# The last pair of sequences is routed to the experts as two single sequences

## The chip, the cores and the metric

One NeuronCore of a Trainium2 chip runs the kernel. Its engines are TensorE (PE; PEld is its weight load), VectorE (DVE), ScalarE (ACT), GpSimd (POOL) and SyncE (SP); each takes its own instructions strictly in order, and semaphores tie them together. The metric is the time on the device in microseconds (us), where less is better. Lines named as L487 are lines of the kernel before; in the changed kernel the same code stands up to eight lines further down.

## The reference, cut to what matters

Eight sequences of 512 tokens with 128 features go through a block with two halves. The first half is a layer norm with a modulation, four Mamba2 layers (a scan over the tokens) and a residual sum. The second half is a mixture of experts, and the change lies in how its input is made:

```python
h = _layernorm(x, axis=-1) * (1 + cb) + sb
...
normed = hidden_states * jax.lax.rsqrt(var + 1e-08) * norm_weight
shared = jnp.maximum(normed @ sw1 + sb1, 0.0) @ sw2 + sb2
flat = normed.reshape(-1, d)
probs = jax.nn.sigmoid(flat @ router_w.T)
scores, idx = jax.lax.top_k(probs, TOPK)
w = scores / (jnp.sum(scores, axis=-1, keepdims=True) + 1e-06)
...
h = jnp.maximum(jnp.einsum('td,edh->teh', flat, ew1) + eb1[None, :, :], 0.0)
eo = jnp.einsum('teh,eho->teo', h, ew2) + eb2[None, :, :]
routed = jnp.einsum('teo,te->to', eo, comb)
return shared + routed.reshape(b, s, -1)
```

Each of the 4096 tokens goes to two of eight experts and to a shared expert. All is float32.

## The kernel before, in words

**The scan.** A loop over `t` walks through the 128 chunks of each engine's work (8 sequences, 4 chunks of 128 tokens, 4 layers), a few steps of lead and of drain on either side. The order of the instructions on every engine is the order in which this loop writes them (`manual_schedule`). The last chunk's result passes L940 (DVE), L944 (ACT), L955 and L959 (PE), L966 (DVE), L967 (POOL, a power) and L975 (DVE, which adds it to the sequence).

**The route.** When the last layer has finished with a pair of sequences, the generator `rejoin(g)` takes the pair `sets[g]` and does all that stands between scan and experts. It is advanced by one `yield` at a time: in the loop once or twice in each step of the drain, so that its instructions lie between those of the scan, and behind the loop as fast as the others allow. Pair `g` begins at the step `t == NC * (U - B) + NC * (seqs[-1] + 1) + 2`, so the four pairs begin at 106, 114, 122 and 130; the scan's last step is 127. One `rejoin` issues in this order:

- L312 to L316: sums of squares on ACT, then a reciprocal square root `power` (L300 to L305), which from the third pair on is 11 small DVE operations;
- L343, L347, L349: scale (ACT), modulation and residual sum (DVE);
- L355 to L365: statistics and a second root (DVE); L368: the layer norm (ACT); L375: its modulation (DVE);
- L312 again and a third root; L385 (ACT): the rows that go to the experts; L389: the token's number; L395: a second copy of them (DVE);
- L394, L398: the rows transposed (PE) and scaled (ACT); L402: the router's matmuls (PE);
- L424 to L446: the two largest of eight (ACT, DVE); L451 to L464: how many tokens of the set and of earlier sets go to each expert, with the running count in `taken`; L461, L462: a row's place among the tokens of its expert (PE);
- L470 to L480 (DVE): weights and the lists of places `ix`. For each chunk and each of the two experts one scatter is put into the list `scatters`.

**The scatters.** L487 (POOL) writes 128 rows of 130 floats to their places in `xg` in HBM. In the drain one goes out at each step, behind the loop all at once. A pair has 16 of them, all four pairs 64. Rows live in the pool `frow` with two buffers as long as the loop runs, and in `frow2`, also with two, behind it; L380 holds a set back until an older one's scatters have gone out.

**Shared expert.** `shared()` computes it for each routed sequence on PE (L562: hidden layer, L540: second layer) and ACT (L529: ReLU, L533: the result). It is advanced by `serve()` between the steps of `rejoin`.

**Tables and tiles.** When all sets are counted, `tables()` sums up the counts of all tokens (L1131 on PE) and computes on DVE (L1134 to L1163) which expert and which rows each of 39 tiles of 256 rows has; L1168 and L1169 pick the tiles' biases. `fetch(j)` on SP reads a tile's two numbers into registers (L1176, L1177), loads the expert's weights (L1179, L1181), its bias (L1184) and then the rows (L1188). The first three tiles' weights are asked for before the rows of any; the rows need every scatter to have landed. Then, tile by tile, `turn` (L1195), `hidden` (L1206) and `combine` (L1219) run. Only POOL's instructions behind the loop are put in order by the tile scheduler and not by hand: they include two IOTA (L1123, L1125) into memory that the scan's tiles have left, and so wait for these.

Of the kernel before, what the change touches and what calls it, by code (L numbers as in the profile page):

```python
# [8 lines left out]
F32 = mybir.dt.float32  # L9
# [6 lines left out]
P = 128  # L16
# [8 lines left out]
def adaln_mamba_moe(  # L25
# [28 lines left out]
    B, L, DM = x.shape  # L54
# [3 lines left out]
    E, _, FH = ew1.shape  # L58
# [55 lines left out]
    scb = const.tile([P, B, P], F32, name="scb")  # L114
# [102 lines left out]
    fp = ctx.enter_context(tc.tile_pool(name="fp", bufs=1))  # L217
# [13 lines left out]
    taken = [fp.tile([P, E], F32, name="taken0")]  # L231
# [54 lines left out]
        yield  # L286

    hTx, scatters, rowpools, banks, held = {}, [], [frow], [], {}
    sets = [(b, b + 1) for b in range(0, B, 2)]
    routed = set()  # L290

    def power(v, name, on_pool):

# [25 lines left out]
    def rejoin(g):  # L319
# [17 lines left out]
        mine = slice(b0 % 2 * NC, b0 % 2 * NC + n)  # L337
# [39 lines left out]
        rs = yield from mean_squares(h, 1e-8, f"G{g}", on_pool)  # L377
        yield

        while scatters and scatters[0][0] in held.get(len(rowpools), [])[:-1]:  # L380
            yield
        held.setdefault(len(rowpools), []).append(g)
        rows = [rowpools[-1].tile([P, G2, RW], F32, tag=f"row{c}", name=f"row{c}_{g}")[:, :n] for c in range(2)]
        for j in range(n):
            nc.scalar.activation(rows[0][:, j, :DM], h[:, j, :], AF.Copy, scale=rs[:, j : j + 1])  # L385
# [4 lines left out]
        for i, b in enumerate(seqs):  # L390
# [6 lines left out]
            hTx[b] = h[:, t, :].rearrange("p s d -> p (s d)")  # L397
            nc.scalar.activation(hTx[b], pt[:, :L], AF.Copy, scale=nw)  # L398
        yield
        pr = banks[-1](f"pr{g}")  # L400
        for j in range(n):
            nc.tensor.matmul(  # L402
# [10 lines left out]
        def t3(tag):  # L413
            return f2.tile([P, G2, E], F32, tag=tag, name=f"{tag}{g}")[:, :n]

        def t2(tag):
            return f2.tile([P, G2], F32, tag=tag, name=f"{tag}{g}")[:, :n]
# [5 lines left out]
        p = t3("prob")  # L423
# [36 lines left out]
        pp = banks[-1](f"pos{g}")  # L460
        nc.tensor.matmul(pp[:, :m], below, mx.rearrange("p s e -> p (s e)"), start=True, stop=False)  # L461
        nc.tensor.matmul(pp[:, :m], ones, before.rearrange("p s e -> p (s e)"), start=False, stop=True)  # L462
        taken.append(fp.tile([P, E], F32, name=f"taken{g + 1}"))
        nc.vector.tensor_add(taken[g + 1], before[:, n - 1, :], mx[:, n - 1, :])  # L464
        den = t2("den")
        nc.vector.scalar_tensor_tensor(den, m1, 1e-6, m2, ALU.add, ALU.add)
# [8 lines left out]
        for c, oh in enumerate((oh1, oh2)):  # L475
            nc.vector.tensor_mul(oh, oh, pos)
            ix = rowpools[-1].tile([P, G2], mybir.dt.uint32, tag=f"ix{c}", name=f"ix{c}_{g}")[:, :n]
            at = t2(f"at{c}")
            nc.vector.tensor_reduce(at, oh, AX.X, ALU.add)
            nc.vector.tensor_copy(ix, at)  # L480
            for j in range(n):
                scatters.append((g, xg, rows[c][:, j, :], ix[:, j : j + 1], "rows"))
        yield

    def scatter(to, of, ix, group):
# [92 lines left out]
    with ExitStack() as actx:  # L578
# [424 lines left out]
        for t in range(-NC * LEAD - EARLY, NI + 4):  # L1003
            p = t + NC * LEAD
# [16 lines left out]
            for g, seqs in enumerate(sets):  # L1021
                if t == NC * (U - B) + NC * (seqs[-1] + 1) + 2:
                    gens["pairs", g] = rejoin(g)
# [76 lines left out]

    fc = ctx.enter_context(tc.tile_pool(name="fc", bufs=1))
    fh = ctx.enter_context(tc.tile_pool(name="fh", bufs=2))
    rowpools.append(ctx.enter_context(tc.tile_pool(name="frow2", bufs=2)))
    fw3 = ctx.enter_context(tc.tile_pool(name="fw3", bufs=4))
    psT = ctx.enter_context(tc.tile_pool(name="psT", bufs=2, space=PSUM))
    psD = ctx.enter_context(tc.tile_pool(name="psD", bufs=3, space=PSUM))
# [237 lines left out]
```

## Time and profile before

| | |
|---|---|
| median of 4 runs | 1167.01 us (1163.3 to 1168.66) |
| the profiled execution | 1169.04 us, span of its instructions 1167.3 us |
| PE, DVE, ACT, POOL busy | 83%, 73%, 65%, 73% of the span |
| scan and drain | up to about 880 us |
| last routes and scatters | about 880 to 973 us |
| 39 expert tiles | about 977 to 1136 us |
| sums and output | to 1167.3 us |

The page gives the busy time of each engine over the whole span. A table by stretch gives, for each stretch of time, the busy time of each engine with the number of instructions in brackets, then the clock of TensorE that was granted (1.00 is full), the share of the DMA engines' time and what they moved. The list in order of time gives start, duration, engine, line, operation, what it writes and reads, and in square brackets how long the engine was idle before it and what ended that; "issue" is idle time in which the engine waited for nothing that the profile shows, and "remote" an end that it can't assign to an instruction just finished.

### The profile page before, as it was taken

The numbers are of one execution on the slowest core, as the hardware profiler recorded it, in microseconds if no ns is written. First come the engines' busy times: TensorE is split into PE (matmuls) and PEld (weight loads), VectorE is DVE, ScalarE is ACT, GpSimd is POOL, SyncE is SP. The second block draws the span as 40 slices with busy tenths as digits, with TensorE's granted clock in tenths as the row PEclk, the third lists the DMA queues.
The fourth block names the chain that finished last, engine by engine and source line by source line (L and its number), as shares of the span: only waits on it lengthen the run. The fifth ranks groups of instructions, "written<-read, shape, count | busy, mean of one in ns | idle before, by whom it ended". The sixth has DMA issues, their size and how long they took to land. (4 is left out here: it accounts for less than half of the span.)

```text
span 1167.3 us, 21562 instructions
## 1 busy us (share of the span) xinstructions
PE 974.2 (83%) x7130; PEld 738.3 (63%) x7130; DVE 855.9 (73%) x2084; ACT 761.4 (65%) x1641; POOL 856.7 (73%) x937
## 2 busy tenths in 40 slices
PE   4657899989989989899899999877685775999985
PEld 2335666666767767667667676656463554888882
DVE  3768878898898788988988888997554352666653
ACT  4766889778888887888788888767434522333320
POOL 6867978889898798898898887998842533555550
PEclk9767989999999999999999999878867986999997
DMA  5141445546455455363233334424100115787756
GB/s 109 4 138 37 137 118 185 158 128 191 131 192 171 129 169 161 118 209 111 86 134 110 106 107 131 148 93 137 33 23 19 37 44 145 218 218 219 211 145 220
DMA packets 134303, 151.19 MB, mean 130 GB/s; under 512 B 22569, under 2 KB 106697, under 8 KB 134193
## 3 DMA queue, kind: packets, MB, share of 16 engines
q1 hardware_dynamic: 127184, 137.91, 40.0%
q0 software_dynamic: 4672, 9.42, 2.4%
q10 hardware_dynamic: 2336, 2.50, 0.7%
q8 instruction: 56, 0.92, 0.3%
q14 instruction: 55, 0.44, 0.1%
HBM read 120.07 MB, written 29.71 MB: 128 GB/s over the span
## 5 line engine op out<-in xcount | busy, mean ns | idle before, releaser
L668 DVE SCALAR_TENSOR_TENSOR xbc<-px,cw,xbc 128x511 f32<-128x511 f32 (+2 forms) x384 | 286.2, 745 | 35.8 <-ACT xbc L658 28.8
L801 POOL TENSOR_TENSOR dV<-dV,cum 128x1024 f32<-128x1024 f32 x128 | 244.3, 1908 | 5.0 <-DVE xbc L668 4.5
L860 DVE TENSOR_TENSOR dV<-dV,ptx 128x1024 f32<-128x1024 f32 x128 | 155.0, 1211 | 18.1 <-ACT xT L838 17.3
L806 POOL TENSOR_SCALAR_AFFINE_SELECT dV<-dV 128x1024 f32<-128x1024 f32 x128 | 142.2, 1111 | 9.3
L487 POOL DMA_INDIRECT yg<-y,ix x78 | 84.1, 1078 | 85.9 <-DVE y L1230 71.5
L817 ACT ACTIVATE dV<-dV 128x1024 f32<-128x1024 f32 x128 | 134.5, 1051 | 13.5 <-POOL dV L806 13.1
L944 ACT ACTIVATE sq<-g 128x256 f32<-128x256 f32 x128 | 53.0, 414 | 119.3 <-DVE g L940 103.4
L646 PE MATMUL px<-hT,Wi 128*128 128x512 f32 x192 | 104.9, 629 | 15.8 <-DVE xbc L668 14.5
L487 POOL DMA_INDIRECT xg<-row,ix x64 | 63.4, 991 | 62.9 <-ACT hds L529 42.1
L658 ACT ACTIVATE xbc<-px,cbias,cw 128x512 f32<-128x512 f32 x128 | 98.5, 769 | 15.0 <-PE px L646 13.4
L844 POOL TENSOR_TENSOR xd<-xT,dt 128x256 f32<-128x256 f32 x128 | 79.2, 618 | 31.8 <-ACT xT L838 31.3
L869 PEld LDWEIGHTS py<-xbc,st 128*128 128x128 f32 x384 | 60.2, 203 | 62.3 <-issue 49.6
L959 PE MATMUL po<-Wo,g 128*128 128x128 f32 x512 | 89.5, 298 | 0.0
L1212 ACT ACTIVATE hd<-ph,bs 128x256 f32<-128x256 f32 x78 | 32.7, 470 | 83.6 <-PE ph L1206 74.6
L928 PE MATMUL py<-dV,xd 128*32 128x128 f32 x2048 | 85.0, 285 | 0.0
L918 PEld LDWEIGHTS py<-xbc,dg 128*128 128x128 f32 x512 | 80.1, 203 | 7.1 <-issue 1.0
L955 PEld LDWEIGHTS po<-ones,sq 128*128 128x128 f32 x512 | 67.8, 193 | 25.7 <-issue 22.9
L918 PE MATMUL py<-xbc,dg 128*128 128x128 f32 x512 | 82.5, 286 | 0.0
L856 PE MATMUL ptx<-xbc 128*128 128x128 f32 x256 | 55.6, 300 | 30.5 <-DVE dV L860 30.0
L955 PE MATMUL po<-ones,sq 128*128 128x1 f32 x512 | 78.2, 257 | 0.0
L1219 PE MATMUL pe<-w,hd 128*128 128x128 f32 x624 | 75.9, 275 | 0.0
L1206 PE MATMUL ph<-xt,w 128*128 128x256 f32 x312 | 75.1, 385 | 0.1
(252 smaller groups left out, 2358.8 us busy)
## 6 DMA issues: line engine op xcount, KB each, us to landing
dV<-crow SPq DMA_DIRECT2D x128, 512.0 KB
w<-in_L_ffn_ew_dram SPq DMA_DIRECT2D x78, 256.0 KB
xg<-blank SPq DMA_DIRECT2D x64, 260.0 KB
ecum<-crow SPq DMA_DIRECT2D x256, 48.0 KB
rows<-xg SPq DMA_DIRECT2D x39, 130.0 KB
b<-in_L_ffn_eb_dram SPq DMA_DIRECT2D x39, 64.0 KB
x<-in_L_attn_x_dram SPq DMA_DIRECT2D x8, 256.0 KB
md<-mods SPq DMA_DIRECT2D x8, 256.0 KB
```

The source lines that it names most:

```text
L487: i = nc.gpsimd.indirect_dma_start(out=to, out_offset=bass.IndirectOffsetOnAxis(ap=ix, axis=0), in_=of, in_offset=None)
L646: nc.tensor.matmul(px[v, k][:, :L], Wi[l][:, c0 : c0 + P], hT[v], start=True, stop=True)
L658: nc.scalar.activation(xbc[v][:, k, :], px[v, k][:, :L], AF.Identity, bias=cbias[:, l, k : k + 1], scale=cw[:, l, k, KT - 1 : KT],)
L668: nc.vector.scalar_tensor_tensor(xbc[v][:, k, d:], px[v, k][:, : L - d], cw[:, l, k, KT - 1 - d : KT - d], xbc[v][:, k, d:], ALU.mult, ALU ...
L801: nc.gpsimd.tensor_tensor(dV[i], dV[i], cums[g][:, h0 : h0 + NH].unsqueeze(2).to_broadcast([P, NH, Q]), ALU.subtract)
L806: nc.gpsimd.affine_select(out=dV[i], in_=dV[i], pattern=[[0, NH], [1, Q]], compare_op=ALU.is_ge, fill=-200.0, base=0, channel_multiplier=-1,)
L817: nc.scalar.activation(dV[i], dV[i], AF.Exp)
L860: nc.vector.tensor_mul(Ms[i], Ms[i], pg.pop(i).unsqueeze(1).to_broadcast([P, NH, Q]))
L918: nc.tensor.matmul(py[i][:, k, :], dg[l][:, k, :], xbc[u][:, k, t], start=False, stop=True, skip_group_check=True,)
L928: nc.tensor.matmul(py[i][j * HD : (j + 1) * HD, k, :], xd[:, h, :], M[:, h, :], start=False, stop=True, skip_group_check=True,)
L955: nc.tensor.matmul(pp[:, 2 * DM + c : 2 * DM + c + 1], sq[:, k, :], ones[:, 0:1], start=(k == 0), stop=(k == NB - 1))
L959: nc.tensor.matmul(pp[:, c * DM : (c + 1) * DM], g[:, k, :], Wo[l][:, k, :], start=(k == 0), stop=(k == NB - 1))
```

## The change

The last two sequences become sets of their own. There are five sets: three pairs, sequence 6 and sequence 7. Set 3 (sequence 6) begins at `t` = 126 and set 4 (sequence 7) at 130, each with four chunks and eight scatters. All that is issued for each set, such as the roots, the search for the two largest, the counts and the lists, is issued once more, on half as many elements for these two sets.

Three places for rows stand in `frow2`, and a set waits for a place until the set that had it is routed and its scatters have gone out. A set also doesn't start its router's matmuls before the set two ahead of it is routed, so that no more than two are in the buffers of `f2` at a time. The running counts `taken[1:]` lie in columns of `scb`, a tile that the scan's entry has left, instead of in tiles of their own. The two loops that wait do so while the program is written: they set the order of the instructions and are not in the program.

```diff
-    sets = [(b, b + 1) for b in range(0, B, 2)]
-    routed = set()
+    sets = [(b, b + 1) for b in range(0, B - 2, 2)] + [(B - 2,), (B - 1,)]
+    routed, done = set(), {-2, -1}
+    scratch = scb.rearrange("p b q -> p (b q)")
...
-        while scatters and scatters[0][0] in held.get(len(rowpools), [])[:-1]:
-            yield
-        held.setdefault(len(rowpools), []).append(g)
+        while True:
+            mine = held.setdefault(len(rowpools), [])
+            full = mine[-1 - len(rowpools)] if len(mine) > len(rowpools) else -1
+            if full in done and full not in [f[0] for f in scatters]:
+                break
+            yield
+        mine.append(g)
         rows = [rowpools[-1].tile([P, G2, RW], F32, tag=f"row{c}", name=f"row{c}_{g}")[:, :n] for c in range(2)]
...
         yield
+        while g - 2 not in done:
+            yield
         pr = banks[-1](f"pr{g}")
...
-        taken.append(fp.tile([P, E], F32, name=f"taken{g + 1}"))
+        taken.append(scratch[:, g * E : (g + 1) * E])
         nc.vector.tensor_add(taken[g + 1], before[:, n - 1, :], mx[:, n - 1, :])
...
                 scatters.append((g, xg, rows[c][:, j, :], ix[:, j : j + 1], "rows"))
+        done.add(g)
         yield
...
-    rowpools.append(ctx.enter_context(tc.tile_pool(name="frow2", bufs=2)))
+    rowpools.append(ctx.enter_context(tc.tile_pool(name="frow2", bufs=3)))
```

What this makes of the order on the engines: on POOL the scatters of the second pair that are still left at the loop's end stand nine (before: ten) ahead of the two IOTA and five behind them, then L967 and two more (before: L967 and then six). Then come 16 scatters of the third pair, eight of sequence 6 and eight of sequence 7. On PE the positions of sequence 6 (L461, L462) stand right behind those of the third pair, and sequence 7's transposition, router and positions follow between blocks of the shared expert. DVE routes sequence 6 ahead of the third pair as far as the two largest, and issues its lists right behind the third pair's. SP's order is unchanged.

## The prediction

> **What bounds the kernel now.** I read the page, then a table by stretch behind the scan, then the waits and the instructions in order of time there. The page shows busy engines, and that is an average over stages: the table shows 923 to 973 us, where nothing is full.
>
> ```profile
> span 1167.3 us, 21562 instructions
> core 0: us, PE busy (x) PEld busy (x) DVE busy (x) ACT busy (x) POOL busy (x), PEclk, DMA share, GB/s
> 913.00:923.00 10.00, 9.52 (x63) 7.26 (x62) 2.95 (x14) 7.64 (x24) 7.67 (x8) 1.00 0.15 47
> 923.00:936.00 13.00, 5.23 (x25) 3.90 (x24) 0.00 (x0) 0.12 (x1) 7.65 (x8) 0.75 0.14 46
> 949.00:957.00 8.00, 7.19 (x64) 7.00 (x63) 7.38 (x26) 1.13 (x2) 6.44 (x6) 1.00 0.13 43
> 957.00:973.00 16.00, 0.00 (x0) 0.00 (x0) 3.18 (x6) 0.58 (x1) 9.57 (x10) 0.60 0.46 127
> 973.00:981.00 8.00, 4.16 (x12) 3.15 (x13) 0.00 (x0) 1.74 (x4) 0.00 (x0) 0.52 0.72 208
> ```
>
> From 923 to 936 PE issues 25 matmul records instead of some 80, and waits for nothing that the profile names ("issue"). The waits and the order of time tell with what this goes:
>
> ```profile
> PE pes L540 <- issue: 7.8, 11, 1.8
> ...
> 877.75 0.16 DVE L966 TENSOR_SCALAR rg<-po 128x2 f32<-128x2 f32 x1 [9.34 <-remote]
> 877.80 0.28 POOL L1123 IOTA ahead<- 128x128 f32 x1 [1.58 <-remote]
> 878.67 0.72 POOL L967 TENSOR_TENSOR rg<-rg,mhalf 128x2 f32<-128x2 f32 x1
> 879.43 0.61 DVE L975 SCALAR_TENSOR_TENSOR h<-po,rg,h 128x128 f32<-128x128 f32 x2 [1.51 <-POOL rg L967]
> 913.04 0.96 POOL L487 DMA_INDIRECT xg<-row,ix  x1 [26.09 <-ACT hds L529]
> 931.98 0.96 POOL L487 DMA_INDIRECT xg<-row,ix  x1 [0.30 <-issue]
> 935.88 0.58 ACT L533 COPY h<-pes 128x512 f32<-128x512 f32 x1 [14.45 <-remote]
> 948.98 0.96 POOL L487 DMA_INDIRECT xg<-row,ix  x1 [16.05 <-ACT hds L529]
> 968.63 0.95 POOL L487 DMA_INDIRECT xg<-row,ix  x1 [0.30 <-issue]
> 972.14 0.58 ACT L533 COPY h<-pes 128x512 f32<-128x512 f32 x1 [18.17 <-remote]
> 973.33 1.36 SPq L1188 DMA_DIRECT2D rows<-xg  x3
> 976.70 1.12 PE L1195 MATMUL pt<-ident,rows 128*128 128x128 f32 x4 [20.51 <-DMA rows<-xg]
> ```
>
> The reader should see a pattern, three times. POOL issues a run of scatters (L487) every 1.26 us; some us into the run nobody sees any more what PE has finished; 1.5 to 2.9 us after the run ends all of it is seen. The matmul that L966 waits for ended at 872.5, the run at 876.2, L966 starts at 877.75; the run 913.04 to 932.94 releases ACT's L533 at 935.88; the run 948.98 to 969.58 releases L533 at 972.14, though its matmuls had ended at 956.2. I call this the hold. It had not begun 4.4 us into the third run (the copy at 953.38 was on time) and had at 7.2 us. PE itself is slow from 11.5 us into the second run, SP's instructions (0.70 us each) from 9.4 us into the third. So the path is: scan's end, third pair's route, 16 scatters, hold, fourth pair's route, 16 scatters, first fetch of expert rows at 973.33. From there 160 us of expert tiles and 31 us of output follow, which the diff leaves alone.
>
> **The change, part by part.**
>
> 1. Sequence 6 starts four steps of the scan earlier. In the changed program's order DVE gets 12 small operations of a square root ahead of the last L860 (started every 0.20 us: 2.4) and one L347 (0.69) ahead of the second pair's index lists, where DVE has no gap: that pair's scatter run begins at 863.29 + 3.1 = 866.4. Its L349, statistics and second root (0.7 + 1.2 + 2.6) lie in DVE's idle 9.34 us before L966; without that they would cost 4.5.
>
> 2. On POOL the order changes around L967: nine scatters instead of ten stand before the two IOTA, and then five more before L967, which they follow now at once. Nine scatters end at 866.4 + 8 x 1.26 + 0.96 = 877.4, the hold's tail of 1.5 makes 878.9, IOTA 0.94, five scatters 6.3, L967 0.75: L975 starts at 887.0 instead of 879.43, so 7.6 later. Queued behind L975 on DVE is the third pair's root (L316 at 879.95), for which ACT's row copies wait, so all of the third pair's route moves. If the nine don't start the hold, 1.3 less.
>
> 3. From L975 to the third pair's first scatter it was 33.6 us. Now sequence 6 also goes through: on PE one transposition (0.44) and four router matmuls (0.93), on DVE its counts and row copy (1.7) ahead of the third pair's lists. What ACT and DVE get besides (row copies, a root) answers to L343 and L375 that go. Between 0, when all lies under other work, and 3.1, when none does, I take 1.5: the run begins at 913.04 + 7.6 + 1.5 = 922.1.
>
> 4. Sequence 6 is routed right behind the third pair, so 24 scatters run without a gap: to 922.1 + 23 x 1.26 + 0.96 = 952.0, and the hold with its tail (2.6, between 1.5 and 2.9) to 954.6. Sequence 7's positions and the count matmul (L1131) stand on PE behind some 12 us of shared-expert work that follows the run's start: inside the hold. What was hidden from 13 us of slow PE now is hidden from some 20.
>
> 5. The tables follow at 954.6 (948.98 to 955.50: 6.5), then sequence 7's lists (L470 to L480 and start, 2.0): its first scatter goes at 963.1, 14 us later than the fourth pair's did, but it has eight: 7 x 1.26 + 0.95 = 9.8, to 972.9. Before: 969.58. So the halved last run saves 10.1 and the start costs 13.4 net.
>
> 6. SP read the table at 955.5 and needed until 973.3 for three fetches at the slow pace, 3.75 after the last scatter. Now it reads at 961.1, the run is too short to slow it for long, and at the pace after 974 (2.8 a tile) it is done by 972; the scatters land 0.9 after their end (970.5 after 969.58). The rows go at 974.0 to 975.5: +0.7 to +2.2, taken +1.0.
>
> 7. PE had nothing from 957 to 976 and the granted clock was 0.52 when the first tiles came; its 16 matmuls L1206 took 5.04, where later eight take 1.73. Now it has from 954.6 still seven L562 (0.86) and 48 L540 (0.22), 16.7 us, and some 3 more at half clock: to 974.5. It stays fast: -1.6. This work hid under the tables before; its cover now is 2.5 us wide.
>
> The third place for rows and the counts kept in an old tile move no instruction, and the new `while` loops are decided while the program is built: no engine waits for them, 0. Sequence 6's load of `mods` (L328) is issued earlier, but SP's order stays the same, nothing is passed: 0. The 68 more rows of small DVE work (0.2 each, 13.6) lie in DVE's empty 923 to 941, apart from what stands in 1 and 3.
>
> Sum: +1.0 - 1.6 = -0.6 us. The profiled execution took 1169.04 (span 1167.3), 2.0 above the runs' median of 1167.01; on the median that is 1166.4.
>
> Two rules of the Trainium skill speak here, and the sum doesn't use them. "SBUF — State Buffer" (section "SBUF: two separate sides") says that DVE copies in a two-port mode keep GpSimd from writing the descriptors of its DMAs, some 620 ns becoming 3100. More DVE work beside a longer run would then cost up to 2.5 us for each of about ten copies, 25 us: an estimate by that page's figures, and it speaks against the change. Here 48 scatters took 954, 958 and 1463 ns (least, median, most), also with DVE busy 7.38 of 8 us: at most 0.5 each. The same page (section "Who interferes with whom") says that a DMA never contends with a compute engine. By that there were no hold, and rival B's time would come; the three runs say otherwise.
>
> **The rivals.** A, slower: PE doesn't get through to L1131 inside the long run. It decides where PE turns slow: before 7.5 us into the run, 44 records are left (32 of L540, 12 beyond); at 0.52 to 0.81 us a record 25 us do 31 to 48 of them. From 5.5 us on, or at the slower pace, 18 to 31 remain, at half clock 0.21 each: +4 to +7 on tables and scatters, and the work left on PE outlasts the rows. 1172. For it: the hold began before 7.2 us; against it: PE kept its pace for 11.5.
>
> B, faster: the hold does not last through a run of 24, or spares L1131. Then POOL alone decides: 32 scatters from 920.6, 31 x 1.26 + 0.96 = 40.0, to 960.6, rows at 961.7, 11.6 earlier, 1155. Against it: three holds out of three lasted to the run's end.
>
> C, nothing reaches the end: the expert tiles, which wait for their rows' DMA for 3.4% of the span (40 us), take up what a microsecond gives or costs: 1167.
>
> **How the numbers follow.** Forecast 0.47 (own range 1163 to 1170: part 3 and the tail of the hold both ways), C 0.08, A 0.29, B 0.16. 0.3% is 3.5 us, about what can be told from no change (the four runs lie 1163.3 to 1168.66). Of the forecast 0.06 falls below 1163.5 and 0.04 above 1170.5; with B and a twentieth of A inside: faster 0.22, same 0.46, slower 0.32. The range takes A whole and leaves most of B out: 1159 to 1174.
>
> **What would show it.** Right: L975 near 887; one run of 24 L487 from about 922; ACT idle to a "remote" release at about 954.6, and the tables' L1134 just behind; a last run of eight ending near 973; L1195 within 3 us of 976.7 at full clock. Wrong: L1134 before the run of 24 ends (B), PE still on L540 ahead of L1131 when it has ended (A), or L975 where it was.

## The result, and the profile after

The changed kernel took 1167.57 us (median of 44 runs, 1159.27 to 1175.53), the kernel before 1164.84 (70 runs, 1158.51 to 1175.48): ratio 1.0024, interval 1.0013 to 1.0034, so 1.5 to 4.0 us slower. The forecast was 1166.4 with 0.46 on "within 0.3%". The time is in the forecast's range, but its sign is wrong: 0.6 us less were forecast, and the change costs a little.

The profiled execution of the changed kernel took 1167.89 us, 0.3 above its median. That of the kernel before took 1169.04, 4.2 above the median over 70 runs (over the four that I had, 2.0). So the difference of the two executions isn't the 2.7 us of the medians: the two traces tell how, and only roughly how much.

In the order of time behind the scan (start, duration, engine, line, operation, in brackets the idle time before it and what ended it; L495 is what was L487, L541 was L533, L974, L975 and L983 were L966, L967 and L975, L1142 was L1134, L1196 was L1188, L1203 was L1195):

```profile
877.11 0.16 DVE L974 TENSOR_SCALAR rg<-po 128x2 f32<-128x2 f32 x1 [4.90 <-PE phs L570]
884.28 0.73 POOL L975 TENSOR_TENSOR rg<-rg,mhalf 128x2 f32<-128x2 f32 x1
885.05 0.61 DVE L983 SCALAR_TENSOR_TENSOR h<-po,rg,h 128x128 f32<-128x128 f32 x2 [7.78 <-POOL rg L975]
919.13 0.96 POOL L495 DMA_INDIRECT xg<-row,ix  x1 [31.62 <-ACT hds L537]
948.19 0.95 POOL L495 DMA_INDIRECT xg<-row,ix  x1 [0.30 <-issue]
953.37 0.58 ACT L541 COPY h<-pes 128x512 f32<-128x512 f32 x1 [22.73 <-remote]
953.54 0.29 DVE L1142 TENSOR_TENSOR full<-pn,ahead 128x128 f32<-128x128 f32 x1 [25.38 <-remote]
961.53 1.21 POOL L495 DMA_INDIRECT xg<-row,ix  x1 [12.39 <-issue]
973.16 0.58 ACT L541 COPY h<-pes 128x512 f32<-128x512 f32 x1 [7.50 <-remote]
974.38 1.36 SPq L1196 DMA_DIRECT2D rows<-xg  x3
976.52 0.66 PE L1203 MATMUL pt<-ident,rows 128*128 128x128 f32 x2 [2.48 <-issue]
```

Here the forecast's picture is found again: the scan's last root L975 behind five scatters, one run of 24 (919.13 to 949.1), in it a hold that ends with two "remote" releases at 953.4, a last run of eight, the rows at 974.38. The table by stretch (stretch and its length, then busy time and number of instructions of each engine, the granted clock, the DMA share) shows PE inside the hold and at the first tiles:

```profile
core 0: us, PE busy (x) PEld busy (x) DVE busy (x) ACT busy (x) POOL busy (x), PEclk, DMA share, GB/s
923.00:931.00 8.00, 7.15 (x39) 4.70 (x38) 3.94 (x23) 2.94 (x5) 6.17 (x7) 1.00 0.17 58
931.00:953.00 22.00, 5.85 (x11) 2.42 (x10) 0.00 (x0) 0.00 (x0) 13.88 (x15) 0.57 0.14 45
974.00:982.00 8.00, 5.25 (x15) 4.03 (x15) 0.40 (x2) 2.37 (x5) 0.00 (x0) 0.57 0.57 147
```

For 12 us into the run PE had kept its pace (39 records in the 8 us up to 931); then come 11 records in 22 us, with DVE and ACT empty. And the last row: where the first tiles come, the granted clock is 0.57.

### The profile page after: what moved, and what is told of

The parts are those of the page before. It is cut to its first block, busy times and chain, and to the rows that moved or that the text cites. A ratio compares the mean times of both kernels' runs of the same rounds, so it can differ in the third digit from the quotient of the medians.

```text
span 1165.9 us, 21643 instructions
## 1 busy us (share of the span) xinstructions
PE 966.9 (83%) x7134; PEld 731.6 (63%) x7134; DVE 864.0 (74%) x2152; ACT 761.6 (65%) x1644; POOL 856.6 (73%) x937
## 5 line engine op out<-in xcount | busy, mean ns | idle before, releaser
L868 DVE TENSOR_TENSOR dV<-dV,ptx 128x1024 f32<-128x1024 f32 x128 | 155.1, 1211 | 19.1 <-ACT xT L846 18.3
L495 POOL DMA_INDIRECT yg<-y,ix x78 | 84.1, 1079 | 83.8 <-DVE y L1238 69.0
L495 POOL DMA_INDIRECT xg<-row,ix x64 | 62.7, 979 | 65.3 <-ACT hds L537 31.6
L967 PE MATMUL po<-Wo,g 128*128 128x128 f32 x512 | 88.9, 297 | 0.0
L1214 PE MATMUL ph<-xt,w 128*128 128x256 f32 x312 | 75.6, 387 | 0.0
```

Of the source, the lines that this page charges most:

```text
L495: i = nc.gpsimd.indirect_dma_start(out=to, out_offset=bass.IndirectOffsetOnAxis(ap=ix, axis=0), in_=of, in_offset=None)
L868: nc.vector.tensor_mul(Ms[i], Ms[i], pg.pop(i).unsqueeze(1).to_broadcast([P, NH, Q]))
L1214: nc.tensor.matmul(ph[:, i, :], w1[:, k * P : (k + 1) * P], xt, start=True, stop=True)
```

## The experiments

All ratios are to the kernel before on the same chip. The runs went to five chips, and these fall into two kinds, which turned out to be the main finding. On two of them (call them holding chips) the kernel before took 1165.2 and 1166.6 us, like the comparison above; on three it took 1147.4 and 1146.7 (one chip, measured twice), 1147.9 and 1145.3. Each experiment below names its kind. To compare traces I count from the start of the scan's last root but one on POOL (860.03 in the kernel before, 860.16 in the changed one), since the scan itself ends up to 7 us earlier or later from one execution to the next. This reference point is good for two kernels that both have the split. Between pairs and the split it hides 2.25 us, because the split puts work of DVE ahead of it. There I count from the root before it, the earlier root (848.33 in the kernel before, 846.20 in the changed one; lines under step 1 below).

**1. The places and counts alone (holding chip).**

```diff
-    sets = [(b, b + 1) for b in range(0, B - 2, 2)] + [(B - 2,), (B - 1,)]
+    sets = [(b, b + 1) for b in range(0, B, 2)]
```

> The changed kernel with four pairs again: the three places for rows, the counts kept in the old tile and the new loops alone are left. My theory: they move nothing, so the time is that of before, 1164.8 (ratio to before 0.999 to 1.001), third pair's run from about 913, L1196 near 973. Rival D, the places themselves cost the 2.8 us (other addresses, other waits): 1167.5, ratio 1.002 or more.

Measured: 1166.18, ratio 0.9987 (0.9964 to 1.001). That part is worth nothing that can be measured, as costed, and the rival D of the expectation falls.

**2. The scan's last root on DVE (holding chips, twice).**

```diff
-                nc.gpsimd.tensor_tensor(rs, rs, mhalf[:, 0:2], ALU.pow)
+                if i == NI - 1:
+                    rs = power(rs, "last", False)
+                else:
+                    nc.gpsimd.tensor_tensor(rs, rs, mhalf[:, 0:2], ALU.pow)
```

> The changed kernel, but the scan's last root is computed on DVE (11 small operations, some 2.3 us) in place of POOL's L975, so it is behind no scatter. My theory: the last add L983 begins near 879.6 in place of 885.05, and as all behind it hangs on it, the run of 24 begins near 913.7, the tables' release comes near 948, L1196 near 969: 5.4 us off 1167.6, 1162. Rival C, the expert tiles take it up: the same rows move, the time stays 1167. A third way: the third pair's route hangs on something else, then the run of 24 stays at 919.

> The changed kernel with the scan's last root on DVE, once more. On a chip without the hold: one run of 32 scatters begins 5.4 us earlier than in the changed kernel (53.0 in place of 57.9 behind the start of L974's root one chunk earlier) and all behind it moves with it: 5 us off 1150.9, 1146, ratio to before 0.999, so that the split by itself gains nearly nothing there. On a chip with the hold: as in the first call, 0.997.

Measured: 1162.32, ratio 0.9973 (0.9951 to 0.9996), and 1163.99, 0.9987 (0.9962 to 1.0012). Against the changed kernel's 1.0024 that is 5.9 and 4.3 us less; 5.4 were expected. The order of time of the second one (its scan root but one started at 857.69; L986 is the add that was L983):

```profile
877.50 0.61 DVE L986 SCALAR_TENSOR_TENSOR h<-po,pylast,h 128x128 f32<-128x128 f32 x2
911.53 0.96 POOL L495 DMA_INDIRECT xg<-row,ix  x1 [27.16 <-ACT hds L537]
945.72 0.58 ACT L541 COPY h<-pes 128x512 f32<-128x512 f32 x1 [23.41 <-remote]
967.17 0.33 SPq L1199 DMA_DIRECT2D rows<-xg  x1
```

The add comes 19.8 behind the reference point in place of 24.9, the run of 24 at 53.8 in place of 59.0, the release at 88.0 in place of 93.2, the rows at 109.5 in place of 114.2: the whole train moves by some 5. So POOL's order around L975 is what makes the change lose on a holding chip; without it the split is, by the two ratios, worth 3.1 and 1.5 us, the second not clear of nothing. (Both kernels have the split, so this comparison doesn't hang on the choice of the reference point.)

**3. The third pair's scatters left out (holding chip), in the kernel before and in the changed one.**

```diff
...
             while scatters:
-                scatter(*scatters.pop(0)[1:])
+                f = scatters.pop(0)
+                if f[0] != 2:
+                    scatter(*f[1:])
```

Not shown are eight DMAs that write zeros to the places of this pair's results during the scan: both kernels leave out the third pair's share of the experts.

> The kernel before with the 16 scatters of the third pair left out: its rows are never routed to the experts, and their places in yg are filled with zeros during the scan, so this part of the output isn't the reference's. My theory of the hold: no slow PE behind 923, so the second layer's copy L533 comes some 13 us before 935.9, the fourth pair's run (16) begins near 936 and is itself followed by a hold until some 959, rows L1188 near 960: 13 us less, 1152. If the hold is no more than something that the profile shows and the time doesn't have, or if the tiles take it up: 1165.

> The same left out of the changed kernel: of the run of 24 the 8 of sequence 6 remain. My theory: 8 scatters (919 to 930) are too short to hold PE for long, so the count matmul comes near 933 and the tables' release near 935 in place of 953.5, the last 8 scatters end near 953, rows L1196 near 956: some 18 us less than 1167.6, 1149, which is 3 less than the kernel before without its third pair. Rival: no hold in the time: 1167.

Measured: 1153.71, ratio 0.9897 (0.9859 to 0.9935), and 1146.61, 0.9829 (0.9793 to 0.9866). Both near the forecast of the hold (1152 and 1149), far from "no hold in the time" (1165, 1167). In the changed kernel without these 16, eight scatters stand alone, and PE's count matmul and DVE's L1150 (the one that was L1142) are nearly on time:

```profile
919.56 0.96 POOL L503 DMA_INDIRECT xg<-row,ix  x1 [33.09 <-issue]
929.83 0.28 PE L1147 MATMUL pn<-scb,ones 128*128 128x8 f32 x2
931.39 0.29 DVE L1150 TENSOR_TENSOR full<-pn,ahead 128x128 f32<-128x128 f32 x1 [4.81 <-PE phs L578]
953.44 0.33 SPq L1204 DMA_DIRECT2D rows<-xg  x1
```

L1150 starts at 931.39 where L1142 was held until 953.54, with the run's start at 919.56 against 919.13. Behind this run of eight the matmul's end is seen 1.3 us late (930.1 to 931.4), behind the run of 24 it was 12.8 us (940.7 to 953.5). POOL stood idle between its two runs in both full kernels (16.05 us in the kernel before, 12.39 in the changed one), so it isn't POOL's own time that was saved. The hold is in the time and not only in the trace, and it goes with the run's length.

**4. The long run broken, by the lists of places.** The third pair's second eight and sequence 6's eight scatters wait until the count of all tokens is on DVE; in the kernel before, the third pair's second eight.

```diff
+            late = g == 3 or (g == 2 and c == 1)
...
-            nc.vector.tensor_copy(ix, at)
+            def counted(zero, ix=ix, at=at, send=send):
+                nc.vector.tensor_add(ix, at, zero.to_broadcast([P, n]))
+                send()
...
+        zero = fc.tile([P, 1], F32, name="zero")
+        nc.vector.tensor_scalar_mul(zero, full[:, 0, 0:1], 0.0)
+        while gated:
+            gated.pop(0)(zero)
```

> The changed kernel with the run of 24 broken: the third pair's first 8 scatters go at once, its second 8 and sequence 6's 8 wait, by their lists of places, until the count of all tokens is there. Nothing is left out. My theory: 8 scatters don't hold PE before the count matmul is through, so it comes near 930; 24 (then 8) scatters follow from some 932 to 962 (sequence 7's right behind or among them), rows L1196 near 963 in place of 974.4: 11.5 us off 1167.6, 1156. Rival: the run's length has nothing to do with it, PE is slow from about 931 as ever: the scatters that wait only lose time, 1172 or more.

> The same breaking in the kernel before, with pairs: the third pair's second 8 scatters wait for the count of all tokens. My theory: PE is not held behind 923, the count matmul comes near 935 (934.7 where the third pair was left out), 24 scatters run from 936 to 966, rows L1188 near 967 in place of 973.3: 6 us off 1164.8, 1158.5. Rival, the scatters only lose time: 1165 or more.

> Both together: the run of 24 broken, and the scan's last root on DVE. Nothing is left out. My theory: the two gains add, as both shift the start of the last uninterrupted run: 5.4 and 11.5 off 1167.6, 1150.7, and faster than the kernel before by 14 (ratio 0.988). If the tiles or PE's left-over work become the end: 1155 or more, with L1196 early and the first transposition waiting on PE.

Measured on a chip of the second kind: 1155.96, 1157.98 and 1146.35 us. The first two are within 0.6 us of the forecasts and mean the opposite: the kernel before took 1147.43 there, so the ratios are 1.0081 (1.005 to 1.0111), 1.0103 (1.0073 to 1.0134) and 0.9994 (0.9977 to 1.0012). What I had not reckoned with: this chip doesn't hold, and the scatters that wait only lose time. The first and the third differ in the scan's last root alone, on POOL or on DVE: its place costs 9.6 us there, and the last add comes 37.1 and 28.1 us behind the earlier root.

**5. Both kernels on the second kind of chip.**

> The kernel before itself, for its trace on the chip of this call. The chips differ: it took 1166.6 on the chip of the first experiments and 1147.4 on that of the second. My theory: the second one doesn't hold PE and SP during a run of scatters. Where this call's chip is like the first: runs of 16 and 16 with a gap of some 17 us, L533 released 2 to 4 us behind the first run, rows L1188 113 us behind the scan's last root L967 but one (860 to 973). Where it is like the second: the fourth pair's run begins near 935 (right behind the third's, 913 to 933), the rows come near 957, 16 us earlier, and no ACT copy is released by a remote end.

> The changed kernel itself. On a chip that holds: as measured, 0.24% slower than before, 1.001 to 1.003. On one that doesn't: POOL alone decides, 32 scatters without a gap from 919.1 (5.6 later than before, behind L975) end at 959.2, rows near 960.3, against 957 in the kernel before: +3.5 us on 1147.4, 1151, ratio 1.003. A rival for such a chip: without the hold the split brings what it is for, rows before 957 and a ratio below 0.999.

> The changed kernel on the same chip as the other two. With the hold: 1.002 to before, release of the tables 93 us behind the start of the scan's last root but one, rows 114 us behind it. Without: 1.003 to 1.004, one run of 32.

> The run of 24 broken and the last root on DVE, again, as the chip of the second experiments seems not to hold and so couldn't show what the breaking is for (0.9994 there). On a chip that holds: 1150.7, ratio 0.988 to before. On one that doesn't: 0.999 as there.

Measured: the kernel before 1151.02 in its profiled execution (1146.68 the median of the 22 runs beside it), the changed kernel 1150.94, ratio 1.0037 (1.0009 to 1.0065), and on another chip of this kind 1154.34, 1.0061 (1.0033 to 1.0088); the broken run with the root on DVE 0.9998 (0.9977 to 1.0019). The kernel before, in order of time and by stretch:

```profile
912.39 0.95 POOL L487 DMA_INDIRECT xg<-row,ix  x1 [25.66 <-ACT hds L529]
936.23 0.95 POOL L487 DMA_INDIRECT xg<-row,ix  x1 [3.94 <-ACT hds L529]
955.87 0.96 POOL L487 DMA_INDIRECT xg<-row,ix  x1 [0.30 <-issue]
958.49 0.33 SPq L1188 DMA_DIRECT2D rows<-xg  x1
```

```profile
923.00:936.00 13.00, 12.96 (x71) 8.97 (x69) 6.41 (x34) 6.59 (x11) 7.15 (x8) 1.00 0.13 42
```

Its row of the table by stretch shows that from 923 to 936 PE works through 71 records; on the holding chip it was 25 in the same stretch. The DMA engines did the same on both, 42 and 46 GB/s: the scatters' data moves no slower on a holding chip. The fourth pair's run follows the third's at 936 and not at 949, and the rows go at 958.49: 96.9 behind the reference point (861.60) in place of 113.3. That is 16.4 of the 18 us between the two kinds of chip. The changed kernel there:

```profile
885.18 0.35 DVE L983 SCALAR_TENSOR_TENSOR h<-po,rg,h 128x128 f32<-128x128 f32 x1 [11.24 <-POOL rg L975]
919.88 0.96 POOL L495 DMA_INDIRECT xg<-row,ix  x1 [32.25 <-ACT hds L537]
931.96 0.29 DVE L1142 TENSOR_TENSOR full<-pn,ahead 128x128 f32<-128x128 f32 x1 [3.73 <-PE pn L1139]
959.24 0.95 POOL L495 DMA_INDIRECT xg<-row,ix  x1 [0.30 <-issue]
961.52 0.33 SPq L1196 DMA_DIRECT2D rows<-xg  x1
```

One run of 32 without a gap, from 919.88 to 960.2; the tables are ready in the middle of it, and the rows wait for POOL alone. The gap of 4 us that the kernel before has between its two runs is gone, but the run begins 71.9 behind the earlier root (848.02) in place of 62.5 (849.88). So the rows come 4.9 later (113.5 in place of 108.6), and 4.5 later in the trace on the other chip, where the times differ by 4.3 and 6.5. The bracket of L983 says whose fault most of it is: 11.24 us behind POOL.

**6. The broken run on a holding chip.**

> The run of 24 broken and the last root on DVE. On a chip with the hold, my theory: the count matmul near 922 to 925, the 24 scatters end near 954, rows near 957, 1150.7, ratio 0.988 to before; rival, the length of the run isn't what holds PE: PE slow 12 us behind the first 8 scatters' start as well, the count comes late and the scatters that wait for it with it, 1165 or more. On a chip without the hold: 0.9996 as twice before.

Measured: 1158.41, ratio 0.9941 (0.9918 to 0.9964): 6.8 us faster than the kernel before, half of what was forecast. The order of time (scan root but one at 862.65):

```profile
916.94 0.96 POOL L508 DMA_INDIRECT xg<-row,ix  x1 [27.64 <-ACT hds L550]
929.46 0.28 PE L1155 MATMUL pn<-scb,ones 128*128 128x8 f32 x2
941.38 0.70 SPq L1207 DMA_DIRECT2D w<-in_L_ffn_ew_dram  x1
944.21 0.70 SPq L1209 DMA_DIRECT2D w<-in_L_ffn_ew_dram  x1
960.53 0.96 POOL L508 DMA_INDIRECT xg<-row,ix  x1 [0.30 <-issue]
968.01 1.36 SPq L1216 DMA_DIRECT2D rows<-xg  x3
```

The length of the run is what holds PE: behind eight scatters the count matmul passes at 929.46 and its reader on DVE starts at 929.85. In the run of 24 of experiment 2 its two halves were issued 1.4 us apart (933.58 and 935.01), and their end was seen 11 us later (945.96). Of what is missing, some 5 us went to SP: its three fetches, begun at 936.9, lay beside the new run of 24 and took until 968, 31 us, and the rows' DMA goes 6.5 us behind the last scatter's end instead of 1.4 as on the other kind of chip. The last scatter itself ended late as well, 112.8 behind the earlier root, where the forecast's 954 stands for 107.8 in the changed kernel's trace from which it was taken. From SP's first DMA to the last before the rows it takes 26.4 us (941.38 to 967.8). On the other kind of chip the same DMAs of the same kernel (the trace of experiment 4), beside the same run, are issued within 7.7 us (first and last):

```profile
931.05 0.37 SPq L1207 DMA_DIRECT2D w<-in_L_ffn_ew_dram  x1
938.39 0.37 SPq L1212 DMA_DIRECT2D b<-in_L_ffn_eb_dram  x1
```

This kernel is the one to keep of those that were run: faster than both on a holding chip, level with the kernel before on the other kind (0.9994 and 0.9998), where the changed kernel is slower.

**7. Two questions that stay open.** Whether fewer fetches ahead of the rows would win back SP's 5 us, and whether on a holding chip it is the scatters' DMAs or POOL's being busy that slows PE:

```diff
-                fetched = [fetch(j) for j in range(3)]
+                fetched = [fetch(j) for j in range(2)]
...
+        fetch(2)()
         turn(0)
```

> The run of 24 broken, the last root on DVE, and only two tiles' weights fetched ahead of the first rows in place of three; the third tile's follow behind the rows. On a chip with the hold: two fetches of some 10 us each are done near the last scatter's end, so the rows go some 6 us earlier than in the run with three (968.0 there): ratio 0.989 to before in place of 0.994. If the third tile's weights come late by as much: 0.994 again. On a chip without: the rows wait for the scatters anyway, and the third tile's weights leave 2.8 us behind them: 1.000 to 1.002.

> The run of 24 broken, the last root on DVE, two tiles' weights ahead of the first rows. With the hold: the rows go at the end of the last scatter, some 6 us earlier than the 968 of the run with three, ratio 0.989; if the third tile's weights come late by as much, 0.994. Without: 1.001 as before.

```diff
...
-                scatter(*scatters.pop(0)[1:])
+                f = scatters.pop(0)
+                if f[0] != 2:
+                    scatter(*f[1:])
+                else:
+                    for _ in range(2):
+                        nc.gpsimd.tensor_scalar_mul(idle, f[2][:, :DM], f[2][:, DM : DM + 1])
```

> The changed kernel, with each of the third pair's 16 scatters replaced by two multiplications on POOL of about 0.6 us each, which send nothing: POOL is as busy as before, with 16 DMAs fewer. Left out as in the runs without the third pair: its rows never reach the experts, zeros stand in their place. If it is the scatters' DMAs that hold PE (my theory): PE works on, the count matmul comes near 930 and the tables' release near 931; sequence 6's eight scatters begin when POOL is free, near 939, the last of sequence 7 ends near 960, rows L1196 near 961, 13.5 us off 1167.6: 1154. If a busy POOL is enough to hold PE: release near 953 as in the changed kernel, 1167.

> The third pair's 16 scatters replaced by multiplications on POOL, as once before (on a chip without the hold, where it could tell nothing of it): that pair's rows never reach the experts, zeros stand in their place. On a chip with the hold: if the scatters' DMAs hold PE, the count matmul and the tables come near 932 (as there) and the time is 12 to 14 us under the changed kernel's; if a busy POOL is enough, the release comes near 953 and the time is the changed kernel's. On a chip without: 1.005 to before, as it was.

> The third pair's 16 scatters replaced by multiplications on POOL, that pair's rows left out and zeros in their place. With the hold: if the scatters' DMAs hold PE, the tables' release comes near 932 and the time is 12 to 14 us under the changed kernel's 1167.6; if a busy POOL is enough, release near 953, 1167. Without: 1.005 as twice before.

All five runs landed on chips that don't hold: ratios 1.0011 (0.9991 to 1.0031) and 1.0014 (0.9994 to 1.0035) for the two fetches, 1.0048 (1.0023 to 1.0074), 1.0057 (1.0034 to 1.008) and 1.006 (1.0039 to 1.0081) for the multiplications. There they show only that two fetches ahead bring nothing, and that 16 multiplication pairs in the scatters' place leave the time where the changed kernel has it: POOL's time is the bound there, whatever POOL does in it. On a holding chip neither was tried.

## Why the prediction was wrong, point by point

Two things failed: step 7, which had PE's clock wrong, and the end of the hold in steps 4 and 6, which made the rows later than forecast. Steps 1, 2, 3 and 5 came true to within a microsecond. To see this, the moments of the changed kernel must be counted from a point that the change doesn't move. The earlier root is one: between it and the last root but one lie 11.70 to 11.72 us in all five traces of pairs, and 13.94 to 13.97 in all fifteen of the split, on both kinds of chip. The kernel before, then the changed one:

```profile
848.33 0.73 POOL L967 TENSOR_TENSOR rg<-rg,mhalf 128x2 f32<-128x2 f32 x1
856.59 1.21 DVE L860 TENSOR_TENSOR dV<-dV,ptx 128x1024 f32<-128x1024 f32 x1
860.03 0.69 POOL L967 TENSOR_TENSOR rg<-rg,mhalf 128x2 f32<-128x2 f32 x1 [9.81 <-DVE before L451]
863.29 1.06 POOL L487 DMA_INDIRECT xg<-row,ix  x1 [2.57 <-DVE oh L476]
```

```profile
846.20 0.73 POOL L975 TENSOR_TENSOR rg<-rg,mhalf 128x2 f32<-128x2 f32 x1
854.46 0.16 DVE L317 TENSOR_SCALAR pvF<-pssF 128x4 f32<-128x4 f32 x1
856.72 1.21 DVE L868 TENSOR_TENSOR dV<-dV,ptx 128x1024 f32<-128x1024 f32 x1
860.16 0.69 POOL L975 TENSOR_TENSOR rg<-rg,mhalf 128x2 f32<-128x2 f32 x1 [12.07 <-DVE before L458]
864.04 1.06 POOL L495 DMA_INDIRECT xg<-row,ix  x1 [3.18 <-DVE oh L483]
```

With 2.13 us added (848.33 less 846.20), the changed kernel's moments stand beside the forecast's, which were counted in the trace of the kernel before:

| moment | kernel before | forecast | measured |
|---|---|---|---|
| second pair's first scatter behind the reference point | 863.29 | 866.4 | 866.2 |
| last add (L983, was L975) | 879.43 | 887.0 | 887.2 |
| third pair's first scatter | 913.04 | 922.1 | 921.3 |
| end of the hold behind that run | 935.88 | 954.6 | 955.5 |
| last run's first scatter | 948.98 | 963.1 | 963.7 |
| last run's end | 969.58 | 972.9 | 973.8 |
| rows' DMA | 973.33 | 974.3 | 976.5 |

Step 1, sequence 6 earlier: 3.1 forecast, 2.9 measured. The root's twelve small operations, from L317 at 854.46, stand ahead of L868 and move it by 2.3; one L348 costs the other 0.6.

Step 2, POOL's order: 7.6 forecast with step 1 in it, 7.7 measured. L974's wait on DVE was 4.90 in place of 9.34, so that the 4.5 us that step 1 puts there did lie in it. Experiment 2 took the root out from behind the five scatters, and 5.1 came back.

Step 3: from L983 to the third pair's first scatter 34.1 us, before 33.6: 0.5 where 1.5 was taken.

Step 4: the run of 24 and the release behind it, as forecast, but the tail was 4.2 us (949.1 to 953.4) and not 2.6, outside the bounds of 1.5 to 2.9. After the two runs of 24 of experiment 2 it was 4.2 as well. The tail grows with the run; I had taken it from runs of 10 and 16.

Step 5: tables and lists 8.0 (8.5 forecast), the eight scatters 10.1 (9.8).

Step 6: the rows' DMA went 2.75 us behind the last scatter's end, where the forecast left 1.4. The reason given, that eight scatters are too short to slow SP for long, holds for its weight DMAs (the last at 970.25), but not for the end of the run: behind it ACT's L541 was released by a remote end at 973.16, and the rows went 1.2 later. On chips that don't hold the rows go 1.3 to 1.7 behind the last scatter. So the rows come 3.2 later than in the kernel before, in place of the 1.0 taken.

Step 7 is the step that failed in kind: "It stays fast: -1.6." PE had work until 974, but with gaps of 0.6 and 1.0 us behind 971 and then 2.5 us with none, and the granted clock fell to half from 975.0 to 981.8. The 16 matmuls L1214 took 5.56 us (before 5.04). In place of the 1.6 gained stands 0.5 lost. The idea itself has a case: in experiment 6 PE works without a gap from 965.3 to 970.1 and the first tile follows 1.4 us later, and there the same 16 take 3.72 us, at a granted clock of 1.00.

With +3.2 for the rows and +0.5 for step 7 the prediction's own sum is +3.7; counted at the first transposition, which comes only 1.9 later because its rows arrived sooner (2.1 us behind their DMA's start in place of 3.4), it is +2.4. The times say 1.5 to 4.0, the forecast said -0.6. How well this fits is in part chance: on holding chips the rows of the two traces of pairs come 125.0 and 129.7 behind the earlier root, and from the rows to the end five traces of whole kernels take 189.4 to 194.0. Against that stand the 2.3 us of DVE's small operations, equal in all twenty traces, and the root's place in POOL's queue, tested on both kinds of chip. The sizes of the tail at the rows and of the clock at the first tile would need the mean over many traces.

The rivals. A did not come: PE issued the count matmul at 939.2, inside the run. C fell in experiment 2: a train that moves by 5 us moves the time by 4 to 6. B, no hold, is the truth on three of the five chips, and its own numbers were right to half a us: 32 scatters from 920.6 to 960.6 and rows at 961.7 forecast, 919.9 to 960.2 and 961.5 measured. But its sign was wrong. I took the hold away from the changed kernel alone; where there is none, the kernel before is without it as well and takes 1147, and against that 1151 is slower. A rival that changes the hardware's behaviour has to be priced on both sides of the comparison.

The Trainium skill, "SBUF — State Buffer", section "Who interferes with whom", says that a DMA never contends with a compute engine. On the second kind of chip the traces agree (71 PE records in 13 us beside a full run of scatters). On a holding chip PE is slow beside the same run (25 and, in the changed kernel, 11 in 22 us); whether the DMAs do that or something that goes with them, no run here shows. Of the same page's price for descriptors blocked by DVE (section "SBUF: two separate sides") nothing is seen on either: in the changed kernel the 32 scatters behind the scan took 954, 958 and 1213 ns (least, median, most) on a holding chip and 954, 958 and 1101 on one of the other kind.

## What to carry to other kernels

Before an instruction of a shared queue is given more company, ask what small operation on the critical path stands in that queue: here 0.7 us of POOL work behind five scatters cost 4 to 6 us, more than the rest of the split won, and 2.3 us on another engine was the cheaper place. A wait that looks like a property of the kernel may be one of the chip: price both kernels with and without it. Count from a point ahead of everything that the change touches: one that lies behind a part of it makes that part vanish, as 2.3 us did here. And where single executions of one kernel differ by more than the effect, the trace shows the mechanism and only repeated times show the sum.

## What the runs showed of the hardware

- Chips of one type differ in whether TensorE and SyncE are slow during a run of indirect DMAs: on two of five they are (the kernel before 1165 to 1167 us), on three they aren't (1145 to 1148). On the first kind the slow phase begins some 7 to 12 us into a run of 16 or 24. How long it outlasts a run goes with the run's length: 1.5 to 1.8 us behind eight scatters (four cases), 2.5 to 3.0 behind 16 (five), 4.1 to 4.2 behind 24 (four). In it SyncE starts the two weight DMAs of a fetch 1.4 to 4.2 us apart instead of 0.5 to 0.6. DVE goes on at its pace: in experiment 6 the operations that pick the tiles' biases take 0.69 to 0.72 and 0.48 us, from 938.17 to 943.1 beside a PE that is already slow, and 0.71 to 0.75 and 0.48 on a chip of the other kind. The profile puts the waits down to "issue" and "remote"; why they are there, and whether it is the chip itself or something around it, no run shows.
- A hold has an aftermath in the clock: in the first experiment's trace (run of 16 to 927.9, release at 930.84) the granted clock stayed at 0.50 until 943.1, 12 us after PE had work again. Its rows of the table by stretch:

```profile
923.00:931.00 8.00, 3.24 (x9) 2.10 (x9) 0.00 (x0) 0.17 (x1) 3.84 (x4) 0.50 0.13 42
931.00:943.00 12.00, 12.00 (x38) 8.90 (x39) 4.61 (x24) 3.87 (x8) 0.00 (x0) 0.50 0.00 0
```

In the first trace of the kernel before it was back to full 4 us after (939.7). That may be one source of the spread from one execution to the next; no run tests it.
